# Attention with TensorE's order written out: products in one run, other pieces placed by stated durations

## The chip, the cores and the metric

The kernel runs on one core of one Trainium2 chip. The metric is the time of one execution on the device, in microseconds (us): the median of 9 runs is 1704.61 us (1700.4 to 1714.43). The engines are TensorE (PE for matmuls and PEld for the loads of their weights), VectorE (DVE), ScalarE (ACT), GpSimd (POOL) and SyncE (SP, which issues most of the DMAs here).

## The reference

Two transformer blocks over 8 sequences of 512 tokens and 256 features, all in float32. Each block is a layernorm, causal attention with 16 heads of 16 features, a residual addition, a second layernorm, a router, a mixture of experts and another residual addition. Block 0 has rotary position codes, 4 key/value heads, and 32 experts of which each token takes 8. Block 1 has 16 key/value heads, 16 experts with 2 per token, and a shared expert besides.

```
x = x + attention0(layernorm(x));  x = x + moe0(layernorm(x))
x = x + attention1(layernorm(x));  x = x + moe1(layernorm(x))
attention: softmax(mask(q k^T / 4)) v, then the output projection
moe:       sum over chosen e of weight_e * down_e(silu(gate_e x) * up_e x)
```

## The kernel before

The program has four stages: attention 0 over the 8 sequences, the experts of block 0, attention 1 over the 8 sequences, and the experts of block 1 with the gathering of results. The change touches the two attention stages.

**A sequence's heads.** In `Attention` (L615) the 16 heads go in 4 groups (index c) of 4 heads. For one group, `scores` (L628) writes the transposed scores of three "banks" of key blocks (index n): block 0 (512 columns per head), blocks 1 and 3 together (384 + 128), and block 2 (256). Its matmuls (L638) use 32 rows of TensorE for each head, so four heads run side by side. All three banks use one and the same PSUM tile `st` of 4 of the 8 PSUM banks, so the next scores can only be written after ScalarE's exponential (L643) has read the last. `mask` (L649) multiplies the diagonal blocks with a triangle on VectorE. `values` (L653) multiplies the probabilities with v (L661, 32 columns of TensorE per head, four heads side by side, a column of ones beside v for the softmax sums) in four steps, one for each key block. Then it copies the sums out of PSUM on VectorE (L667), transposes them (L674, tile `ot`), and divides (L677, L678) into `otok`.

**The order.** `steps` (L684) is a generator with 6 steps for a group, 24 for a sequence. At each step it makes one scores bank or one piece of the group's `values` generator; the products trail the scores, so that the steps of one group are spread between the next group's scores. `pipeline` (L734) runs the steps of sequence b, and at each of them takes pieces of two other generators: `before(b + 1)`, the next sequence's layernorm, transposes (`turned`, L302: `xT`) and projections (in stage 0 the transposes of the input `xin` at L1251, then `qkv` at L843 with the rotary products on VectorE at L850 to L865, then the transposes `qT`, `kT`; in stage 1 `v` at L941, `q` at L954, `k` at L959); and `finish(b - 1)`, the last sequence's output projection (`oT` L719, `y` L727, addition L731), layernorm, `xT_f`, router (`lg` L321, `rk` L368 and L370) and, in stage 1, the shared expert (`sg` and `su` L402, `sy` L415). The pieces are spread evenly by their number over the steps. A `yield` ends a piece. What follows is the order in which the program traces its instructions; the framework's own scheduler then chooses each engine's order from it, with estimated durations. On the chip each engine runs that order as it stands.

**What the pieces carry to other queues.** At the end of the router's piece, POOL issues the scatters of the layernormed rows to the experts' slabs (L385: 32 for each sequence in stage 0, 8 in stage 1). They read the tile `xn_rows`, which has 2 buffers in stage 0 and 1 in stage 1, so the layernorm of a later sequence waits until they have landed. In stage 1, `ahead1` (L1418) fetches the x of sequence b + 3 through SP during sequence b and issues 32 gathers on POOL (L1200), a pair for each call of `next(early)`; it needs a buffer of x that is free when an earlier sequence is kept (`keep_x`, SP). Weights of the experts are loaded by SP in the same places.

**The experts' stages** already have TensorE's order written out (`tc.manual_schedule`, L1173 to L1179).

Of the kernel before, what the change touches and what calls it, by code (L numbers as in the profile page):

```python
# [72 lines left out]
STEPS = 2 * len(BANKS)  # L73
# [17 lines left out]
def two_blocks_kernel(  # L91
# [78 lines left out]
    def biases1(tmp, bank):  # L170
# [8 lines left out]
        yield  # L179
# [18 lines left out]
        yield  # L198
# [98 lines left out]
    def free():  # L297

        for _ in range(4):
            yield  # L300

    def turned(xn, lnp, bank, name):  # L302

        xT = lnp.tile([P, ND, T], F32, tag="xT", name=f"xT_{name}")
        for c in range(ND):
# [4 lines left out]
            yield  # L310
        return xT

    def ffn_parts(smp, bank):
        def route(n, b, xn, xT, name, again):
# [10 lines left out]
            yield  # L325
# [11 lines left out]
            yield  # L337
# [10 lines left out]
            yield  # L348
# [15 lines left out]
            yield  # L364
# [26 lines left out]
            yield  # L391

        def shared(w, xT, x, name):

            hs = smp.tile([P, NS, T], F32, tag="hs", name=f"hs_{name}", bufs=1)
            for n in range(NS):
# [11 lines left out]
                yield  # L408
            for half_ in range(NT // 2):
# [11 lines left out]
                yield  # L421
# [193 lines left out]
    class Attention:  # L615
# [6 lines left out]
        def __init__(self, n, late, ptp, ps, bank, wo, masked=None):  # L622
            self.n, self.fine, self.late, self.ptp, self.ps, self.bank, self.wo = n, fines[n], late, ptp, ps, bank, wo
            self.heads, self.otok, self.rec = {}, {}, {}
            self.last = iter(())
            self.masked = masked

        def scores(self, b, c, n, probs):  # L628
# [13 lines left out]
            pt = self.ptp.tile([P, NG, width], F32, tag="p2" if n == 2 else "p01", name=f"p_{name}", bufs=1 + (n < 2))  # L642
# [10 lines left out]
        def values(self, b, c, probs):  # L653
# [4 lines left out]
            for step, j in enumerate((0, 1, 3, 2)):  # L658
# [6 lines left out]
                yield  # L665
            osb = late.tile([P, T], F32, tag="osb", name=f"osb_{name}", bufs=1)
            nc.vector.tensor_copy(osb, o)  # L667
            yield
# [4 lines left out]
            for t in range(NT):  # L673
                nc.tensor.transpose(ot[:, t * P : (t + 1) * P], osb[:, t * P : (t + 1) * P], ident)  # L674
# [7 lines left out]
            yield  # L682

        def steps(self, b):  # L684

# [4 lines left out]
            for c in range(NCK):  # L690
                probs = {}
                for n in range(len(BANKS)):
                    self.scores(b, c, n, probs)
                    next(self.last, None)
                    yield
                    if n == len(BANKS) - 1:
                        self.last = self.values(b, c, probs)
                    next(self.last, None)
                    yield
                    self.mask(n, probs)  # L700

        def flush(self):
            for _ in range(STEPS - 1):
                next(self.last, None)
                yield

        def output(self, b, x):
# [8 lines left out]
            for k in range(ND):  # L716
# [4 lines left out]
                yield  # L721
            for h in range(NT // 2):
# [9 lines left out]
                yield  # L732

    def pipeline(att, before, after, n_before, n_after, till, ahead=None, lead=0):  # L734
# [8 lines left out]

        n_steps = NCK * STEPS
        n_after += 4
        drain(before(0))
        for b in range(NB):
            pre = before(b + 1) if b + 1 < NB else iter(())
            post = finish(b - 1) if b else iter(())
            early = ahead(b + 3) if ahead and b + 3 < NB else iter(())  # L750
            made_pre = made_post = 0
            for n, _ in enumerate(att.steps(b)):
# [932 lines left out]
```

## Time and profile before

| | |
|---|---|
| median of 9 runs | 1704.61 us |
| profiled execution, its own time | 1705.27 us |
| its span, from the first to the last instruction | 1703.5 us |
| mean granted TensorE clock | 0.961 |
| attention 0, first exponential of the first sequence to that of the last | 32.7 to 355.8 us |
| first expert transposes of block 0 | 425 us |
| attention 1, first exponential of the first sequence to that of the last | 888.6 to 1329.9 us |
| first expert transposes of block 1 | 1428 us |

The page gives each engine's busy time; the answers by window give the same for a stretch of the span. The columns of such a row are the stretch, its length, then busy time and instruction count of PE, PEld, DVE, ACT and POOL, then the granted clock of TensorE, the DMA share and GB/s. In what follows the stretches run from the first exponential of one sequence to that of the next, so that their length is the period of a sequence. A row of waits names the engine, its tile and line, what it waited for, and then the total, the number of waits and the longest one.

### The profile page before, as it was taken

What the parts mean: (1) busy time and instruction counts of PE and PEld (TensorE: products, weight loads), DVE (VectorE), ACT (ScalarE), POOL (GpSimd) and SP (SyncE); (2) the same over time, 40 slices, a digit from 0 to 9 for tenths busy, and PEclk for the clock granted to TensorE, in tenths of its full rate; (3) what the DMA queues carried; (4) which work ended last, traced back from release to release, by engine and by line L of the source; (5) the groups of instructions that cost most, each with busy time, mean ns of one, the idle gap of its engine ahead of it and who ended that gap; (6) DMA issues with size and microseconds to landing.
All of it is one profiled execution on the core that took longest, in us unless ns stands there. A gap on an engine that the chain in (4) does not pass through costs nothing. (4 is left out here: it accounts for less than half of the span.)

```text
span 1703.5 us, 30922 instructions
## 1 busy us (share of the span) xinstructions
PE 1548.7 (91%) x10180; PEld 1030.7 (61%) x10180; DVE 992.5 (58%) x3131; ACT 650.2 (38%) x865; POOL 795.9 (47%) x660
## 2 busy tenths in 40 slices
PE   5899999995999999999988999989899888999982
PEld 2355544543898999988853455445444445777761
DVE  5687887875554555555555764754656544444452
ACT  2555554552232333333334454454455331222221
POOL 0026767577710004888888548888511011000473
PEclk9999999997999999999999999999999988999996
DMA  2035557236988768999984245664312024343563
GB/s 73 13 88 154 163 167 265 100 140 197 308 262 271 202 201 220 273 261 274 271 188 69 45 107 82 125 138 69 83 52 79 26 86 156 107 156 119 157 226 120
DMA packets 255129, 259.45 MB, mean 152 GB/s; under 512 B 80212, under 2 KB 235988, under 8 KB 254964
## 3 DMA queue, kind: packets, MB, share of 16 engines
q1 hardware_dynamic: 199172, 167.88, 32.3%
q0 software_dynamic: 55296, 88.65, 22.8%
q8 instruction: 88, 1.44, 0.3%
q10 hardware_dynamic: 496, 0.85, 0.2%
q14 instruction: 77, 0.63, 0.1%
HBM read 132.70 MB, written 124.57 MB: 151 GB/s over the span
## 5 line engine op out<-in xcount | busy, mean ns | idle before, releaser
L1200 POOL DMA_INDIRECT x_a<-yg,yrows x256 | 404.5, 1580 | 277.8 <-DMA xg_m<-xg 181.2
L385 POOL DMA_INDIRECT xg<-xn_f,rows_f x320 | 323.5, 1011 | 413.4 <-DVE rows_f L382 197.2
L643 ACT ACTIVATE p_a<-st_a 128x2048 f32<-128x2048 f32 (+1 forms) x192 | 306.0, 1594 | 280.5 <-PE st_a L638 244.2
L1131 PE MATMUL gu_m<-gw,xgTs_m 128*128 x1552 | 335.9, 360 | 4.9 <-DVE xgTs_m L1108 3.0
L1131 PEld LDWEIGHTS gu_m<-gw,xgTs_m 128*128 128x128 f32 x1552 | 258.1, 192 | 34.2 <-DVE xgTs_m L1108 3.3
L1162 PE MATMUL y_m<-dw,hTs_m 96*128 (+1 forms) x952 | 237.7, 379 | 0.0
L638 PE MATMUL st_a<-qT_a,kT_a 32*128 32x512 f32 (+3 forms) x2048 | 203.2, 479 | 11.2 <-ACT p_a L643 11.0
L661 PE MATMUL o_a<-p_a,v 128*32 128x512 f32 (+3 forms) x2048 | 197.6, 455 | 6.7 <-DVE p_a L649 6.6
L649 DVE TENSOR_TENSOR p_a<-p_a,causal 128x512 f32<-128x512 f32 x256 | 170.4, 684 | 56.8 <-ACT p_a L643 55.9
L1108 DVE COPY xgTs_m<-xgT_m 128x512 f32<-128x512 f32 x194 | 133.8, 690 | 109.9 <-PE xgT_m L1106 109.6
L1167 ACT COPY ys_m<-y_m 128x512 f32<-128x512 f32 x194 | 113.6, 585 | 188.9 <-PE y_m L1162 171.7
L1123 DVE SCALAR_TENSOR_TENSOR h_m<-h_m,xg_m,gu_m 128x96 f32<-128x96 f32 (+1 forms) x388 | 114.9, 326 | 117.4 <-ACT h_m L1136 70.5
L1162 PEld LDWEIGHTS y_m<-dw,hTs_m 96*128 96x128 f32 (+1 forms) x952 | 165.2, 190 | 15.1
L1262 POOL DMA_INDIRECT g<-yg,yrows x64 | 65.1, 1017 | 203.3 <-DVE h_m L1123 171.9
L638 PEld LDWEIGHTS st_a<-qT_a,kT_a 32*128 32x128 f32 x2048 | 90.2, 189 | 107.0 <-issue 51.7
L1152 DVE COPY hTs_m<-hT_m 96x256 f32<-96x256 f32 (+1 forms) x194 | 92.8, 479 | 97.0 <-PE hT_m L1151 96.4
L1106 PE MATMUL xgT_m<-ident,xg_m 128*128 128x128 f32 x776 | 120.1, 277 | 15.1 <-DMA xg_m<-xg 12.1
L1139 ACT ACTIVATE h_m<-gu_m 128x192 f32<-128x192 f32 x150 | 49.5, 330 | 211.3 <-PE gu_m L1131 203.2
L1106 PEld LDWEIGHTS xgT_m<-ident,xg_m 128*128 128x128 f32 x776 | 96.1, 142 | 39.2 <-issue 14.8
L661 PEld LDWEIGHTS o_a<-p_a,v 128*32 128x32 f32 x2048 | 49.6, 110 | 108.8 <-issue 67.1
L1151 PE MATMUL hT_m<-ident,h_m 128*96 128x128 f32 (+1 forms) x476 | 84.6, 274 | 0.4 <-DVE h_m L1123 0.4
L667 DVE COPY osb_a<-o_a 128x512 f32<-128x512 f32 x64 | 44.0, 687 | 53.9 <-PE o_a L661 53.7
(198 smaller groups left out, 1690.9 us busy)
## 6 DMA issues: line engine op xcount, KB each, us to landing
yg<-ys_m SPq DMA_DIRECT2D x194, 256.0 KB
xg_m<-xg SPq DMA_DIRECT2D x300, 144.0 KB
xg_m<-xg SPq DMA_DIRECT2D x88, 136.0 KB
xg<-zeros SPq DMA_DIRECT2D x66, 144.0 KB
xg<-xn_f,rows_f POOLq DMA_INDIRECT x320
xg<-zeros SPq DMA_DIRECT2D x34, 136.0 KB
xf<-in_x_dram SPq DMA_DIRECT2D x8, 512.0 KB
x_after<-x_in SPq DMA_DIRECT2D x8, 512.0 KB
```

The costliest lines, as they stand in the source:

```text
L385: inst = nc.gpsimd.indirect_dma_start(out=lay.xg, out_offset=bass.IndirectOffsetOnAxis(ap=rows[:, t, i : i + 1], axis=0), in_=xn[:, t, :], ...
L638: nc.tensor.matmul(st[:, g, at : at + T - j * P], kT[r, j * P : (j + 1) * P], qT[r, j * P :], start=True, stop=True,)
L643: nc.scalar.activation(pt, st[:, :, :width], AF.Exp, scale=SCALE)
L649: self.masked = nc.vector.tensor_tensor(d, d, causal.unsqueeze(1).to_broadcast([P, NG, P]), ALU.mult).ins
L661: nc.tensor.matmul(o[32 * g : 32 * g + 32, j * P :], v1[:, j, v_at + g * (DH + 1) :][:, :32], probs[n][:, g, at : at + T - j * P], start=( ...
L1106: nc.tensor.transpose(tr[:, j, c, :], xg[:, j, c * P : (c + 1) * P], ident)
L1108: nc.vector.tensor_copy(xT, tr)
L1123: nc.vector.scalar_tensor_tensor(h[:, j, :], h[:, j, :], xg[:, j, D:][:, bass.ds(offs[part, i + j][2], 1)], gus[j][:, inner:], ALU.mult, A ...
L1131: nc.tensor.matmul(gus[j], xT[:, j, c, :], gu[:, bass.ds(at + c * 2 * inner, 2 * inner)], start=(c == 0), stop=(c == ND - 1),)
L1162: nc.tensor.matmul(y[:, j, :], hT[:n_in, q, j, :], dn[:n_in, bass.ds(at + q * D, D)], start=(q == 0), stop=(q == n_ch - 1),)
L1167: nc.scalar.copy(ys, y)
L1200: nc.gpsimd.indirect_dma_start(out=xs[b][:, t, :], out_offset=None, in_=yg, in_offset=rows, compute_op=ALU.add)
```

## The change

- The steps of a sequence become 12 gaps (4 groups of 3 banks). In gap 0 of a group TensorE gets the scores of bank 0 and behind them all four products of the group before, in one run (`products`); in gap 1 the scores of bank 1 and the `ot` transposes (`normalize`); in gap 2 the scores of bank 2. The copy of the products out of PSUM moves from VectorE to ScalarE. The tile of probabilities of banks 0 and 1 gets 3 buffers in place of 2.
- Each piece of `before` and `finish` yields a duration. Negative ones stand for waiting and bring no work. A class `Fill` shares a part's total over its gaps by fixed shares and takes pieces while a part is behind or a gap has less than a least amount of work (`LEAST`).
- `finish(b - 1)` begins in gap 2 of sequence b and ends in gap 1 of sequence b + 1. The gathers of `ahead` are called twice in each gap from gap 2, in place of once in each of 24 steps.
- In stage 1 the shared expert's pieces go between the router's, and `qT` and `kT` become single tiles with 3 buffers.
- The whole attention pipeline traces under `tc.manual_schedule(engines={ENG.PE})`, so TensorE's order is the program's; the other engines' orders are still chosen by the framework's scheduler.

```diff
-STEPS = 2 * len(BANKS)
+NGAP = NCK * len(BANKS)
+LEAST = (0.0, 1.6, 1.2)
...
     def free():
         for _ in range(4):
-            yield
+            yield -0.75
...
-            pt = self.ptp.tile([P, NG, width], F32, tag="p2" if n == 2 else "p01", name=f"p_{name}", bufs=1 + (n < 2))
+            pt = self.ptp.tile([P, NG, width], F32, tag="p2" if n == 2 else "p01", name=f"p_{name}", bufs=3 if n < 2 else 1)
...
-                yield
-            osb = late.tile([P, T], F32, tag="osb", name=f"osb_{name}", bufs=1)
-            nc.vector.tensor_copy(osb, o)
-            yield
+            self.osb = late.tile([P, T], F32, tag="osb", name=f"osb_{name}", bufs=1)
+            nc.scalar.copy(self.osb, o)
+
+        def normalize(self, b, c, probs):
...
                 for n in range(len(BANKS)):
                     self.scores(b, c, n, probs)
-                    next(self.last, None)
-                    yield
-                    if n == len(BANKS) - 1:
-                        self.last = self.values(b, c, probs)
-                    next(self.last, None)
+                    if self.last:
+                        (self.products, self.normalize, lambda *_: None)[n](*self.last)
                     yield
                     self.mask(n, probs)
+                self.last = (b, c, probs)
...
+    class Fill:
+        def __init__(self, part, total, share, first, last):
+            self.part, self.total, self.first, self.last = part, total, first, last
+            whole = sum(share[k % len(BANKS)] for k in range(first, last + 1))
+            self.share = [total * s / whole for s in share]
+            self.gap = -1
+            self.at = self.due = 0.0
+            self.waits = False
+        def pass_gap(self, n):
+            self.gap += 1
+            if self.gap >= self.first:
+                self.due += self.share[n]
+        def behind(self):
+            return (self.due - self.at) / self.total
+        def able(self):
+            return self.part and self.gap >= self.first and (self.behind() > 0.0 or not self.waits)
+        def make(self):
+            cost = next(self.part, None)
+            if cost is None:
+                self.part = ()
+                return 0.0
+            self.waits = cost < 0.0
+            self.at += abs(cost)
+            return max(cost, 0.0)
...
+        with tc.manual_schedule(engines={ENG.PE}):
+            drain(before(0))
+            fills = []
+            for b in range(NB):
+                if b:
+                    last = NGAP + 1 if b + 1 < NB else NGAP - 1
+                    fills.append(Fill(finish(b - 1), t_after(b - 1), share, 2, last))
+                if b + 1 < NB:
+                    fills.append(Fill(before(b + 1), t_before, share, 0, NGAP - 2))
+                early = ahead(b + 3) if ahead and b + 3 < NB else iter(())
+                for k, _ in enumerate(att.steps(b)):
+                    filled = 0.0
+                    for fill in fills:
+                        fill.pass_gap(k % len(BANKS))
+                    while True:
+                        able = [f for f in fills if f.able()]
+                        if not able:
+                            break
+                        fill = max(able, key=lambda f: f.behind())
+                        if fill.behind() <= 0.0 and filled >= LEAST[k % len(BANKS)]:
+                            break
+                        filled += fill.make()
+                    for fill in [f for f in fills if f.gap > f.last]:
+                        drain(fill.part)
+                        fills.remove(fill)
+                    if k > 1:
+                        next(early, None)
+                        next(early, None)
+                drain(early)
+            for fill in fills:
+                drain(fill.part)
+            att.flush()
+            drain(finish(NB - 1))
...
-        pipeline(att, before, after0, 15, 12, 22)
+        pipeline(
+            att, before, after0, 12.7, lambda b: 13.5 + (b == 1) + 5.0 * (b == SPLIT[0] - 1), (0.05, 0.55, 0.4)
+        )
...
-                yield from route(1, b, xn, xT, name, False)
-                yield from shared(w1["s"], xT, xs[b], name)
+                routed, beside = route(1, b, xn, xT, name, False), shared(w1["s"], xT, xs[b], name)
+                for made in (routed, beside, routed, routed, beside, routed, routed):
+                    yield next(made)
+                drain(routed)
+                yield from beside
...
-            pipeline(att, before, after1, 15, 17, NCK * STEPS, ahead1, 4)
+            pipeline(
+                att, before, after1, 15.1, lambda b: 29.2 + 4.0 * (b == SPLIT[1] - 1), (0.25, 0.42, 0.33), ahead1
+            )
```

The other yields carry these durations: `xin`, `xT`, `oT`, `qT`, `kT` and each step of the experts' tables 0.5; `qkv` 1.4; halves of `y` and `v`, and each `q` and `k` 1.75; `lg` 1.9; `rk` with the scatters 0.3; a shared expert's `sg` and `su` 3.5, half of `sy` 2.6; waits of 0.6 after `xT`, 1.0 after `oT`, 0.4 between the router's pieces on VectorE, and four times 0.75 for a layernorm.

## The prediction

> **What bounds the kernel now.** I first read the waits by stage, then the rows by window (a sequence from its first exponential to the next one's), then TensorE in order of time. The chain of what ended last reaches back only to 1665 us, into the gathering of results, which the change leaves alone.
>
> ```profile
> 76.10:121.10 45.00, 42.59 (x374) 22.69 (x375) 37.20 (x136) 25.17 (x25) 3.61 (x3) 1.00 0.25 66
> 167.40:213.50 46.10, 43.66 (x388) 23.18 (x388) 37.36 (x136) 25.29 (x24) 32.52 (x33) 1.00 0.51 159
> 262.20:312.00 49.80, 47.09 (x374) 23.99 (x370) 34.07 (x130) 25.36 (x25) 28.80 (x28) 0.97 0.58 200
> 312.00:355.80 43.80, 43.59 (x392) 23.04 (x389) 39.47 (x146) 25.19 (x24) 32.65 (x32) 1.00 0.37 130
> ```
> ```profile
> 1060.94:1123.99 63.05, 61.14 (x420) 31.57 (x419) 39.24 (x127) 31.09 (x28) 52.37 (x36) 1.00 0.60 115
> 1123.99:1193.62 69.63, 63.66 (x420) 33.21 (x419) 39.39 (x127) 31.10 (x29) 57.74 (x40) 0.95 0.59 111
> ```
> PE is busy nearly all of each sequence; POOL fills up in attention 1. The last two rows have the same work: the 6.6 us between them are a wait of xT_f (4.96 us, at 1151.11) and a clock of 0.95.
>
> ```profile
> PE xT_f L308 <- DVE xn_f L292: 14.9, 6, 6.2
> ...
> DVE xn_f L292 <- DMA xg<-xn_f,rows_f: 9.5, 2, 5.4
> ```
> These waits are of attention 1 (935 and 890 to 1330): TensorE waits for xn_f, and xn_f waits for the scatter of the sequence before, whose source it overwrites.
>
> ```profile
> 167.29 1.06 PE L661 MATMUL o_a<-p_a,v 128*32 128x384 f32 x14
> 168.29 0.65 PE L1251 MATMUL xin<-ident,xf 128*128 128x128 f32 x4
> 168.87 0.64 PE L661 MATMUL o_a<-p_a,v 128*32 128x256 f32 x8
> 169.44 0.66 PE L1251 MATMUL xin<-ident,xf 128*128 128x128 f32 x4
> 170.03 1.15 PE L638 MATMUL st_a<-qT_a,kT_a 32*128 32x384 f32 x16
> 171.11 0.66 PE L674 MATMUL ot_a<-ident,osb_a 128*128 128x128 f32 x4
> 171.69 1.07 PE L661 MATMUL o_a<-p_a,v 128*32 128x512 f32 x8
> 172.69 0.66 PE L719 MATMUL oT_a<-ident,otok_a 128*128 128x128 f32 x4
> 175.58 0.30 PE L719 MATMUL oT_a<-ident,otok_a 128*128 128x128 f32 x1 [2.24 <-DVE otok_a L678]
> ```
> Read the starts: four transposes between products take 0.58 us. Within a run they follow at 0.107 (0.43 for four), 256-column matmuls at 0.2145. So each stretch of whole-array work between four-head pieces costs 0.15 to 0.2 beyond its columns.
>
> **The terms.** On PE: scores 1.07, 1.08 and 0.64 (start to start). Products alone 1.00 (512 columns), 0.78, 0.36 and 0.57 (256); 384 and 128 joined take 1.00, so a join saves 0.14 and the run of four takes 2.71 - 0.42 = 2.3. A y or v half, q or k 1.72; qkv 1.28; lg 1.8; sg with su 3.43; sy half 2.6; 0.43 for four transposes; 0.2 for each whole-array stretch. A gap can't be shorter than its exponential lets the one score tile come free: scores, 0.2, exponential (1.88, 1.88, 1.02 by its rows), 0.1: 3.24, 3.24, 1.95.
>
> Working the placement rule by hand with the change's own durations gives the gaps of a full sequence (longer of the two limits).
> Attention 0: 4.0 (half xin), 3.24, 1.95 (two oT), 3.4, 5.6 (two xT, half y, a qkv), 3.8 (half y, a qkv), 3.4, 4.3 (two qkv), 2.1 (three of xT, qT, kT), 3.4, 4.4 (lg and the other two), 1.95: 41.5 us. Six such sequences now take (355.8 - 76.1)/6 = 46.6.
> Attention 1: 3.4, 4.3 (half sy), 4.3 (oT, xT_a, half y), 7.0 (half v, half y), 3.4 (half v), 3.4 (xT_f, q), 5.6 (lg), 6.9 (sg/su, k), 6.0 (q, sg/su), 5.3 (k), 5.4 (rk, sg/su), 3.4 (half sy): 58.4, against 63.05.
>
> **What goes.** oT's wait of about 2.1 a sequence (otok queued behind a layernorm): otok now comes a gap earlier. The products' waits for the mask (PEld, 23.8 us over 50 waits in all): scores and three products now lie ahead of the late one. What is late next is in the following terms.
>
> **New waits, attention 0.** TensorE takes each piece in its place, and behind a late one stand the next scores, hence ACT and DVE too.
> (a) Two qkv stand in gap 7, qT in gap 8. From the end of y on, VectorE owes a layernorm (5.0 us when alone: y ends 1395.5, xT_f starts 1400.60), three rotary tiles at 1.75, one mask 0.62, rec and otok 0.6: 11.5 us, while PE gets from y to qT in 9.2. I take 2.3, with 0 (rotary ahead of the layernorm) and 5 (masks in front, the 39.47 row's load) as ends.
> (b) lg directly behind xT_f waits for two copies (0.584 each) that stand behind an exponential: 1.8 in every second sequence, 0.9; ends 0 and 1.8.
> (c) xT_a three gaps after its layernorm, and small ones: 1.1 (the tables' small steps of sequence 4 among them); ends 0 and 3.
> Sum 45.8 a sequence, 0.8 less than now, 5 us over six. The first sequence has little to fill: 36.3 by gaps and 2 of (a), against 43.4: 5 us less. The last: 2.5 less. Attention 0: **-12.5**.
> The osb copy's move takes 0.69 x 4 from VectorE and gives 0.59 x 4 to ACT, which is idle 45% of a sequence; it must end before ot, about 1.1 us after the products. If it doesn't, 0 to 0.6 a group, inside (c)'s end. The third probability tile lets the exponential of bank 0 run before the products free the first; without it gap 0 would take 2.3 more. qT and kT with 3 buffers only free sooner; TensorE's order hides that either way.
> POOL's 32 scatters take 42 us a sequence (32 x 1.3), so 45.8 still covers them; with two xn_rows buffers a lag has a sequence of slack. SP's weight loads move with the scatters, for a stage that begins after 400 us: nothing, and at most the 8 us of the first xg load if they were late.
>
> **Attention 1.** (d) xT_a, y behind four ACT copies in gap 2: 1.2 (0 to 2.5). (e) xT_f stands one gap (4.3 us) behind y, the layernorm needs 5.0 alone and some 2 of v additions and masks come between: 3 (1 to 5).
> The first sequence has 40.2 by gaps and 1 of waits, against 46.1: -5. The second 57.3 + 4.2 against 63.1: -1.6.
> Sequences 2 to 5 are bound by POOL. From 1004.6 to 1219.9 it runs without a pause: three times 32 gathers at 1.9 (1.6 and 0.3 of issue) and 8 scatters at 1.3, 214 us. They begin 6.7 us after sequence 2's start (997.9), when sequence 0's x is kept. In the new order that is kept in gap 1 of sequence 2 and the fetch goes out in gap 2, so they begin at some 13 (estimate: gap 2 starts at 7.7, keep and fetch 5.3); 15 of 16 pairs still precede the scatter, so it ends at 13 + 214 - 4 = 223 (now 222). xT_f of sequence 4 follows at 225.5 (now 224.1), then 35 of sequence 5 remain (now 41): sequence 6 starts 260.6 after sequence 2, against 265.4: -4.8. TensorE's gain in these sequences becomes waiting for POOL.
> Sequence 6: 64 with the tables against 66.6; the last +1 (its layernorm has no cover); the drained tail -3, since sg/su now stands where rk waited (2.81 us). Attention 1: **-16**.
> ACT's table loads (1.283 each, 30 now) rise to about 42, as three silus each stand between exponentials: 15 us of ACT, beside 31 of 63 busy; only gap 11 (3.7 against 3.4) shows it, 0.3 a sequence, inside (d).
>
> Sum: 1705.3 (the profiled execution, 1703.5 of span) - 28.5 = 1677; the median of the runs, 1704.6, is 0.7 lower.
>
> [...] The row first: the clock was 1.00 in the sequence with a wait of 2.24 us and 0.95 in that with 4.96, where 1.6 us went beyond the wait. [...]
>
> **Rivals.**
> 1. *The waits are covered* (VectorE's scheduler puts rotary tiles first): attention 0 41.5 a sequence, -31 - 7 - 2.5 = -40; attention 1 without (d) and (e), sequences 2 to 5 still held by POOL, -6 - 6 - 5 - 5 - 3 = -25: **1640**. For it: VectorE is idle 8 us of 46. Against: it is late exactly where two qkv and a layernorm meet.
> 2. *VectorE late in the fixed order, slower*: (a) 5, (b) 1.8, (c) 2, and 1.5 of clock for each long idle time: 51.8 a sequence, +23 in attention 0; (e) at 5 in four sequences, -8 in attention 1: **1720**. It decides when the three waits pass 9 us a sequence. For it: VectorE is busy 39.47 of 43.8 in the fastest sequence.
> 3. *No change in time*: the waits come to what switching saves, 1704.
>
> **Chances.** Forecast 0.46 (own range 1660 to 1696), rival 1 0.20, rival 2 0.24, rival 3 0.10. The range takes in most of rivals 1 and 2: 1638 to 1722. No change means within 0.3%, 5 us, what a measurement tells here: faster 0.44 + 0.20 + 0.02 = 0.66, same 0.08, slower 0.26.
>
> **What would show it.** Attention 0's period about 46, its gaps 0 and 3 near 3.4; qT waiting for the rotary sum (kr, qr) on VectorE; xT_f in attention 1 waiting 3 us in early sequences and more behind POOL; L1200 starting some 13 us into sequence 2; the experts' stages unchanged. I would be wrong if VectorE's order puts a layernorm's writing of xn, which itself waits for POOL, ahead of masks, or if the periods fall to 41.

## The result and the profile after

The changed kernel takes 1719.33 us in the median of 10 runs (1716.6 to 1723.4), the kernel before 1703.25 in 31: a ratio of 1.0089 with a 95% interval of 1.0074 to 1.0104. It is 16 us slower, where 28 less were forecast, and it ends at the time of the second rival (1720). The profiled executions are 1705.27 and 1716.86 us (spans 1703.5 and 1715.1); every stretch below is from their traces, from start to start.

Cut at the first and last scores of each attention and at the experts' first transposes and last matmul, the two spans are (us):

| stretch | before | after | difference | forecast |
|---|---|---|---|---|
| to the first scores | 31.5 | 30.5 | -1.0 | 0 |
| attention 0, first to last scores | 361.0 | 360.3 | -0.7 | -12.5 |
| tail of attention 0, to the experts | 32.9 | 40.0 | +7.1 | no term |
| experts 0 | 443.3 | 444.9 | +1.6 | 0 |
| from the experts to attention 1's first scores | 17.8 | 21.8 | +4.0 | no term |
| attention 1, first to last scores | 493.9 | 502.1 | +8.2 | -13 |
| tail of attention 1 | 47.9 | 42.9 | -5.0 | -3 |
| experts 1 and results | 275.4 | 272.6 | -2.8 | 0 |

Two stretches that cost 11 us had no term at all, and both attentions miss what was forecast for them. A single stretch is no better known than to some 3 us: the two runs below that keep one attention in exactly the instruction order of before took 364.4 us for attention 0 and 490.4 for attention 1. Rows by sequence of the changed kernel (columns as in the rows of before: stretch and length, then busy time of PE, PEld, DVE, ACT, POOL, then the granted clock):

```profile
72.00:117.75 45.75, 41.25 (x368) 23.25 (x368) 34.65 (x123) 27.28 (x29) 0.00 (x0) 0.95 0.23 58
117.75:161.60 43.85, 40.90 (x376) 23.41 (x378) 33.56 (x124) 27.25 (x28) 25.92 (x25) 0.97 0.46 142
256.40:308.60 52.20, 45.33 (x368) 24.09 (x367) 32.74 (x123) 27.49 (x29) 34.98 (x35) 0.89 0.63 215
308.60:355.90 47.30, 42.62 (x376) 23.92 (x375) 35.59 (x132) 27.23 (x28) 28.58 (x28) 0.93 0.30 107
1066.70:1134.50 67.80, 61.23 (x420) 33.47 (x424) 37.34 (x124) 35.96 (x34) 56.21 (x39) 0.95 0.61 114
1134.50:1205.00 70.50, 63.84 (x420) 35.05 (x422) 37.32 (x124) 36.06 (x34) 58.30 (x41) 0.90 0.58 110
```

PE's busy time did fall: 41.25 us in the first of these, 42.59 in the row of before, and 42.62 in the last of attention 0 against 43.59. Over the six full sequences of attention 0 it fell by 0.7 to 3.0 us each, which fits the pieces in one go saving switches. But five of these six sequences got longer (45.0, 46.4, 49.8, 43.8, 63.1 and 69.6 us before), and the clock, 0.95 to 1.00 in them before, is now 0.89 to 0.97. TensorE is less busy, waits more, and runs slower. The waits of the changed kernel, and below them one of the kernel before (who waits for whom: us in all, times, longest):

```profile
PE xT_f L311 <- DVE xn_f L293: 36.4, 18, 6.9
PE st_a L642 <- ACT p_a L647: 30.4, 24, 3.0
...
PE qT_a L921 <- DVE qr_a L905: 7.4, 7, 1.6
...
PE lg_f L325 <- ACT xT_f L312: 4.5, 6, 1.0
```

```profile
PE st_a L638 <- ACT p_a L643: 11.0, 12, 3.0
```

The wait for scores by way of the exponential (`st_a`) was 11.0 us in 12 places before, `xT_f`'s 30.2 in 11. `qT_a`'s wait is new, and `lg_f`'s was 0.3 in one place.

### The profile page after: what moved, and what is told of

Same layout as the page of the kernel before. It is cut to its first block, busy times and chain, and to the rows that moved or that the text cites. A ratio compares the mean times of both kernels' runs of the same rounds, so it can differ in the third digit from the quotient of the medians.

```text
span 1715.1 us, 30906 instructions
## 1 busy us (share of the span) xinstructions
PE 1526.8 (89%) x10180; PEld 1048.9 (61%) x10180; DVE 959.4 (56%) x3067; ACT 704.0 (41%) x943; POOL 793.8 (46%) x660
## 3 DMA queue, kind: packets, MB, share of 16 engines
q0 software_dynamic: 55296, 88.65, 22.5%
## 5 line engine op out<-in xcount | busy, mean ns | idle before, releaser
L665 PE MATMUL o_a<-p_a,v 128*32 128x512 f32 (+3 forms) x2048 | 164.8, 466 | 0.0
L665 PEld LDWEIGHTS o_a<-p_a,v 128*32 128x32 f32 x2048 | 60.2, 116 | 129.0 <-issue 116.5
L1155 PE MATMUL xgT_m<-ident,xg_m 128*128 128x128 f32 x776 | 120.1, 277 | 16.1 <-DMA xg_m<-xg 12.0
L1200 PEld LDWEIGHTS hT_m<-ident,h_m 128*96 128x96 f32 (+1 forms) x476 | 58.5, 125 | 18.9 <-issue 7.5
```

The costliest lines, as they stand in the source:

```text
L665: nc.tensor.matmul(o[32 * g : 32 * g + 32, j * P :], v1[:, j, v_at + g * (DH + 1) :][:, :32], probs[n][:, g, at : at + T - j * P], start=( ...
L1155: nc.tensor.transpose(tr[:, j, c, :], xg[:, j, c * P : (c + 1) * P], ident)
L1200: nc.tensor.transpose(hp[:n_in, q, j, :], h[:, j, lo : lo + n_in], ident)
```

## Experiments

The first four ran on a chip on which the kernel before took 1702.87 us. All later ones came to chips on which it took 2010 to 2029 us ("disturbed" in what follows; what is known of it stands at the end); their ratios stand to the kernel before on the same chip, and there only stretches are read that the disturbance leaves alone.

**Which stage loses.** Two kernels with one attention in the changed order and the other exactly as before, down to each engine's order of instructions.

```diff
# new_in_a0: attention 1 keeps the pipeline and classes of before
-            pipeline(att, before, after1, 15.1, ..., (0.25, 0.42, 0.33), ahead1)
+            pipeline_old(att, before, after1, 15, 17, NCK * STEPS, ahead1, 4)
# new_in_a1: attention 0 keeps them
-        pipeline(att, before, after0, 12.7, ..., (0.05, 0.55, 0.4))
+        pipeline_old(att, before, after0, 15, 12, 22)
```

> Attention 0 in the changed order, attention 1 wholly as before. Theory 'the ends': in the profiled executions the last scores of attention 0 come 1.6 us earlier than before, and from the last scores to the experts' first transposes it takes 39.9 us against 32.9, so this kernel is 5 to 6 us slower than before (ratio 1.003 to 1.004), with the whole loss in that drained tail. Rival 'late VectorE in the sequences': the loss of the changed kernel (about 16 us by the medians) lies in attention 0's sequences and this kernel shows most of it, 10 us or more. Rival 'attention 1 alone': no difference from before within 3 us.

> Attention 1 in the changed order, attention 0 wholly as before. Theory 'the ends and POOL': 4 us more before the first scores (the layernorm of sequence 0), 8 us more over the sequences (POOL's gathers start at 16.8 us into sequence 2 instead of 6.7), 5 us less in the drained tail: 6 to 9 us slower than before (ratio 1.004 to 1.005). Rival 'attention 0 alone': no difference within 3 us. If the two stages add up, this kernel and the one with attention 0 alone changed come to some 12 to 16 us together.

Measured: 1709.72 us, ratio 1.0043 (1.0026 to 1.0060), and 1713.14, ratio 1.0049 (1.0032 to 1.0066). The first has its sequences at 360.9 us and its tail at 40.0: attention 0's whole loss is the tail. The second has 21.7 before attention 1, 504.9 in it, 43.3 behind it. The profile of the second is of its longest run, 1719.44 us. The losses by ratio, 0.43 and 0.49%, add up to the whole, 0.89%, within their intervals; neither stage alone is the cause.

**The tail of attention 0.** TensorE before the change, from the last scores on (start, busy time, engine, line, operation; in brackets the idle time and what ended it):

```profile
392.11 0.71 PE L638 MATMUL st_a<-qT_a,kT_a 32*128 32x256 f32 x8 [1.05 <-ACT p_a L643]
392.83 1.07 PE L661 MATMUL o_a<-p_a,v 128*32 128x384 f32 x16
394.69 0.64 PE L661 MATMUL o_a<-p_a,v 128*32 128x256 f32 x8 [0.79 <-DVE p_a L649]
396.15 0.66 PE L674 MATMUL ot_a<-ident,osb_a 128*128 128x128 f32 x4 [0.82 <-DVE osb_a L667]
...
398.11 3.69 PE L727 MATMUL y_a<-wo,oT_a 128*128 128x256 f32 x16
407.29 2.12 PE L308 MATMUL xT_f<-ident,xn_f 128*128 128x128 f32 x8 [5.49 <-DVE xn_f L292]
```

and after it:

```profile
390.44 0.71 PE L642 MATMUL st_a<-qT_a,kT_a 32*128 32x256 f32 x8
393.93 0.21 PE L372 MATMUL rk_f<-chosen,upper 128*128 128x32 bf16 x2 [2.78 <-DVE chosen L354]
...
395.76 0.19 PE L374 MATMUL rk_f<-before_f,ones 128*128 128x32 bf16 x1 [0.71 <-DVE before_f L367]
395.88 4.50 PE L665 MATMUL o_a<-p_a,v 128*32 128x512 f32 x32
401.13 0.66 PE L680 MATMUL ot_a<-ident,osb_a 128*128 128x128 f32 x4 [0.76 <-ACT osb_a L670]
...
404.01 3.29 PE L731 MATMUL y_a<-wo,oT_a 128*128 128x256 f32 x14 [0.24 <-ACT oT_a L723]
412.25 2.21 PE L311 MATMUL xT_f<-ident,xn_f 128*128 128x128 f32 x8 [4.96 <-DVE xn_f L293]
```

Before, the first products follow the scores at once. After, sequence 6's ranking stands ahead of them and waits 2.78 us for VectorE's choice of experts, then 0.71 for a sum; and the 32 products take 4.50 us where they take 2.36 elsewhere. The granted clock was 0.50 from 394 to 400.5 us, and 1.00 in the same place before (392 to 402 us). `ot` comes 10.4 us behind the last scores instead of 3.7, and everything down to the experts hangs on it.

The first attempt to undo that missed:

```diff
+            att.flush()
             for fill in fills:
                 drain(fill.part)
-            att.flush()
```

> The changed kernel with the last group's products and normalization put ahead of what is left of the sequence before it, in both stages. Theory 'the ends': in the tail of attention 0 TensorE stood 2.78 us at the ranking of sequence 6 with the last products queued behind it, and ot came at 401.1 instead of some 396; the tail gets 5 us shorter, that of attention 1 0 to 2 us, so 5 to 7 us less than the changed kernel (ratio to before 1.005 to 1.006). Rival 'the clock': the products were slow for a lowered clock after an idle time, and the idle time only moves; the tail of attention 0 stays within 2 us of 39.9.

Measured: 1719.78 us, ratio 1.0087, tail 40.2. The expectation failed for a plain reason: the ranking had already been made within the last gap, so nothing was left for the flush to pass. The next edit keeps it out of that gap as well:

```diff
-                    last = NGAP + 1 if b + 1 < NB else NGAP - 1
+                    last = NGAP + 1 if b + 1 < NB or att.n == 0 else NGAP - 1
...
+            att.flush()
             for fill in fills:
                 drain(fill.part)
-            att.flush()
```

> The changed kernel with one piece moved in attention 0's drained tail: the ranking of sequence 6 (which waits for VectorE's choice of experts) comes behind the last group's products and normalization instead of ahead of them. (The run before this that put the flush first moved nothing there: the ranking had already been made in the last gap.) Theory 'idle and clock': of the tail's 40.0 us 6 to 7 are the ranking's waits (2.8 and 0.7) and products that then run at 4.5 us for 32, twice their usual 2.3; the products now start 0.7 us after the last scores as before the change, and the tail falls to 33 to 35. As sequence 6's logits then stand directly behind their transposes in gap 10, 0 to 2 us come back in the sequences: 4 to 6 us less than the changed kernel in all. Rival 'VectorE': the products wait for the last mask, which VectorE makes after the choice of experts; the tail stays above 38.

It ran on a disturbed chip (ratio 1.0095, 1.0057 to 1.0132; in a repeat 1.0064, 1.0037 to 1.0092). There the tail as a whole can't be read, since the kernel before with other buffers takes 61.5 and 63.6 us for it on such chips instead of 32.9. But up to the last of `y` the new order without this edit takes 16.0 to 17.1 us there in seven profiles, as on the first chip (16.1):

```profile
608.87 0.91 PE L642 MATMUL st_a<-qT_a,kT_a 32*128 32x256 f32 x8
609.71 3.80 PE L665 MATMUL o_a<-p_a,v 128*32 128x512 f32 x32
614.28 0.66 PE L680 MATMUL ot_a<-ident,osb_a 128*128 128x128 f32 x4 [0.77 <-ACT osb_a L670]
...
617.26 3.29 PE L731 MATMUL y_a<-wo,oT_a 128*128 128x256 f32 x14 [0.24 <-ACT oT_a L723]
```

The products start 0.5 us behind the last scores and the last of `y` 11.0 (repeat: 0.6 and 10.8), against 5.1 and 16.1 in the changed kernel and 0.4 and 9.0 before. So 5 of the 7 us go with the order, as theory had it; the products still take 3.8, at a granted clock of 0.56 (609 to 611 us). The rival, that the products wait for the last mask, fell.

> The same kernel as the run before with the ranking behind the last products, on a chip whose instruction and data transfers aren't slowed. On the slow chip the products started 0.5 us behind the last scores and y ended 11.3 us behind them (changed kernel: 16.3). Theory 'idle and clock': the tail falls from 40.0 to 35 to 36, 4 to 5 us less than the changed kernel in the profile, less 0 to 2 in the last sequence. Rival 'VectorE': above 38.

That transfers were slowed on the disturbed chips is a guess of this and later expectations; what the traces show of it stands at the end.

**The start of attention 1.** VectorE after the change, behind the experts' last copies, and the transposes that wait for it:

```profile
874.64 0.74 DVE L288 BATCH_NORM_STATS2 stats_a<-x_a 128x6 f32<-128x256 f32 x2
...
880.51 1.01 DVE L830 MEMSET v<- 128x1148 f32 x1 [0.19 <-issue]
...
882.64 1.23 DVE L293 TENSOR_SCALAR xn_a<-x_a,mv_a,rstd_a 128x256 f32<-128x256 f32 x4
```

```profile
882.93 2.33 PE L311 MATMUL xT_a<-ident,xn_a 128*128 128x128 f32 x8 [6.91 <-DVE xn_a L293]
```

In the new order sequence 1's first work is made in gap 0, ahead of the first mask, so its layernorm has the same release as sequence 0's; VectorE alternates between the two (the trace from 876.5 on). Besides, its order now has two memsets of `v` ahead of `xn_a` (880.5 and 881.7), which before stood behind it (`xn_a` at 871.9, the first memset at 873.6). `xn_a` begins 8.0 us behind the first statistics instead of 4.3; 2.3 of these 3.7 us are the memsets. `xT_a` waits 6.91 us, where it waited 3.35 before:

```profile
872.37 1.53 PE L308 MATMUL xT_a<-ident,xn_a 128*128 128x128 f32 x8 [3.35 <-DVE xn_a L292]
```

The edit makes that first work from gap 1 on, behind the mask:

```diff
-                    fills.append(Fill(before(b + 1), t_before, share, 0, NGAP - 2))
+                    fills.append(Fill(before(b + 1), t_before, share, int(att.n == 1 and b == 0), NGAP - 2))
```

> The changed kernel with sequence 1's first work in attention 1 (its layernorm) made in gap 1 instead of gap 0 of sequence 0, so behind the first mask. Theory 'two layernorms share VectorE': in the changed kernel the statistics of sequences 0 and 1 have the same release and alternate on VectorE from 874.6 on, and xT_a waits 6.91 us instead of 3.35; with sequence 1's behind the first mask, the stretch from the experts' last matmul to the first scores falls from 21.8 to 17.8 to 19, 3 to 4 us less. Rival 'the two memsets and x': VectorE's memsets of the v tiles (1.01 us each, ahead of xn_a) and the layernorm itself hold it: 21 or more, no gain.

```profile
1150.09 2.43 PE L311 MATMUL xT_a<-ident,xn_a 128*128 128x128 f32 x8 [3.65 <-DVE xn_a L293]
```

Measured: 2023.40 us, ratio 1.0076 (1.0050 to 1.0103). The stretch falls to 17.7 us (other kernels in the new order without the edit, same kind of chip: 20.3 to 21.7; the kernel before with other buffers: 18.1 and 19.0), the wait to 3.65. That is the 4 us. The edit took both causes away at once, since with it the memsets stand behind `xn_a` again:

```profile
1149.62 1.51 DVE L293 TENSOR_SCALAR xn_a<-x_a,mv_a,rstd_a 128x256 f32<-128x256 f32 x4
1151.32 1.01 DVE L830 MEMSET v<- 128x1148 f32 x1 [0.19 <-issue]
```

So the rival was wrong that no gain would come, but right that the memsets hold `xn_a`: theirs is the larger share, and only their place ahead of it goes back to sequence 1's early layernorm. (In the kernel with only attention 0 changed the stretch was 19.1, so some 1 us of it varies by itself.)

**The sequences of attention 0.** TensorE in gap 10 of sequence 1 and on into the next:

```profile
109.31 1.04 PE L311 MATMUL xT_f<-ident,xn_f 128*128 128x128 f32 x8
111.37 2.24 PE L325 MATMUL lg_f<-rw,xT_f 128*128 128x32 f32 x16 [1.01 <-ACT xT_f L312]
113.53 0.87 PE L642 MATMUL st_a<-qT_a,kT_a 32*128 32x256 f32 x8
115.59 2.09 PE L642 MATMUL st_a<-qT_a,kT_a 32*128 32x512 f32 x8 [1.18 <-ACT p_a L647]
117.61 3.91 PE L665 MATMUL o_a<-p_a,v 128*32 128x512 f32 x32
```

The logits wait 1.01 us for ScalarE's copy of `xT_f`, the small scores come late, so their exponential is late, so the next scores wait 1.18; and then scores and products run at half speed (2.09 for eight scores, 3.91 for 32 products). The clock in these stretches:

```profile
109.00:114.50 5.50, 4.31 (x36) 3.36 (x35) 2.56 (x6) 3.01 (x4) 0.00 (x0) 0.95 0.00 0
114.50:117.75 3.25, 2.16 (x12) 0.66 (x16) 3.03 (x21) 1.04 (x3) 0.00 (x0) 0.50 0.00 0
117.75:120.50 2.75, 2.75 (x16) 0.65 (x18) 0.87 (x2) 1.88 (x1) 0.00 (x0) 0.50 0.02 6
120.50:123.25 2.75, 2.75 (x41) 1.70 (x34) 0.49 (x2) 1.08 (x2) 0.00 (x0) 0.95 0.00 0
```

Sequence 2 is the control within the same trace: by the placement rule one `qT` and one `kT` stand around its logits, the copy is done in time, and about the same wait for the exponential costs no clock (granted 1.00 from 154 to 167 us):

```profile
158.44 0.71 PE L642 MATMUL st_a<-qT_a,kT_a 32*128 32x256 f32 x8
160.40 1.14 PE L642 MATMUL st_a<-qT_a,kT_a 32*128 32x512 f32 x8 [1.24 <-ACT p_a L647]
161.47 1.80 PE L665 MATMUL o_a<-p_a,v 128*32 128x512 f32 x17
```

Gap 10, gap 11 and the next gap 0 together, from exponential to exponential: 14.3, 14.2, 14.4 and 14.1 us in sequences 1, 3, 5 and 6, each with a wait of 1.01 and the clock at 0.50 behind it, and 10.2 in sequence 2. (Before: 9.5 to 10.0. Sequence 4, whose gaps hold the experts' tables besides, took 15.2, and 12.4 before.) The edit gives the logits a place of their own:

```diff
             xT = yield from turned(xn, lnp, bank, name)
+            yield -0.8
             yield from route(0, b, xn, xT, name, False)
```

> The changed kernel with a waiting place of 0.8 between xT_f and the logits in attention 0, so that by the placement rule the logits of sequences 1, 2, 3 stand in gap 11, a gap behind their transposes, instead of directly behind them in gap 10. Theory 'logits behind the copies': where both stand in gap 10 it takes 5.55 to 6.4 us from exponential to exponential instead of 3.96, the next scores then wait 1.5 for a late exponential, and the clock falls (products 0.4 us apart instead of 0.2) into the next gap 0; the sequences concerned get 2 to 3.5 us shorter, attention 0 8 to 12 us in all (360.3 to 348 to 352). Rival 'the wait moves': the exponential chain or the ranking, now a gap later, holds TensorE instead, and attention 0 stays within 3 us of 360.3.

```profile
114.59 1.04 PE L311 MATMUL xT_f<-ident,xn_f 128*128 128x128 f32 x8
116.17 0.71 PE L642 MATMUL st_a<-qT_a,kT_a 32*128 32x256 f32 x8 [0.54 <-ACT p_a L647]
116.81 2.07 PE L325 MATMUL lg_f<-rw,xT_f 128*128 128x32 f32 x16
118.81 1.14 PE L642 MATMUL st_a<-qT_a,kT_a 32*128 32x512 f32 x8
119.88 2.36 PE L665 MATMUL o_a<-p_a,v 128*32 128x512 f32 x32
```

```profile
117.00:120.00 3.00, 3.00 (x28) 2.18 (x31) 1.49 (x4) 1.32 (x3) 0.00 (x0) 1.00 0.00 0
120.00:122.00 2.00, 2.00 (x32) 0.77 (x29) 1.93 (x18) 1.88 (x1) 0.00 (x0) 1.00 0.04 8
```

The logits stand behind the small scores, only the small scores still wait, 0.54 us, the clock stays at 1.00, and the three gaps take 9.7 us. In the six profiles with this edit, alone or with the others, they take 9.7 in sequences 3 and 5 throughout, and in sequence 1 four times (11.4 twice); without it on the same kind of chip 14.4 and 14.2 in sequences 1 and 3. Sequence 1, which no scatter disturbs, takes 43.3, 43.8 and 43.8 us in the three runs of this edit and 43.3 to 43.7 in three of the four edits together, against 45.8 to 47.3 in ten profiles of the new order without it. Attention 0 as a whole: 560 to 566 us with the edit alone, 569 to 584 in six profiles without it on such chips, 13 us less by their means. The ratios were 1.0054 (1.0024 to 1.0085), 1.0010 (0.9991 to 1.0029) and 1.0032 (1.0012 to 1.0052); the other single edits had 1.0076 to 1.0095, 1.0036 to 1.0064 and 1.0068 on the same three chips. The rival, that the wait only moves, fell. How much of the 13 us an undisturbed chip gives wasn't measured; the first trace's own control puts it at four times 4 us.

> The logits' place alone. Theory: attention 0 takes 347 to 352 us instead of 360.3, with gap 10 at 2.7 in sequences 1, 3, 5 and 6, and nothing else changes: ratio to before 1.002 to 1.004. Rival 'the wait moves': attention 0 within 3 us of 360.3, ratio 1.008 or more.

**POOL in attention 1.** From the trace's rows of POOL, and of SP's keep and fetch of x:

```
                 sequence 2   x kept at   gathers from   third scatter ends   sequence 6
before                997.9      997.5         1004.6               1219.9       1263.3
after                1004.0     1013.9         1020.8               1233.7       1274.7
gathers from gap 0   1005.1          -   (no pause: 32 follow on the ones before, to 1028.7)   1285.0
```

```profile
1013.86 0.34 SPq L161 DMA_DIRECT2D x_after<-x_a  x1
1016.54 0.34 SPq L164 DMA_DIRECT2D x_a<-x_after  x1
```

Sequence 0's x is kept 9.9 us into sequence 2, when its last addition is done; keep and fetch take 7.0 more, and the gathers begin 16.8 us into the sequence instead of 6.7. The obvious cure:

```diff
-        xs[b] = xpool.tile([P, NT, D], F32, tag="x", name=f"x_{name}_{b}", bufs=5)
+        xs[b] = xpool.tile([P, NT, D], F32, tag="x", name=f"x_{name}_{b}", bufs=6)
...
-                    if k > 1:
-                        next(early, None)
-                        next(early, None)
+                    next(early, None)
+                    next(early, None)
```

> The changed kernel with the fetch of x and the gathers of attention 1 from gap 0 of a sequence instead of gap 2 (and a sixth buffer for x, so that the fetch needn't wait for x of an earlier sequence to be kept). Theory 'POOL sets sequences 2 to 5': the gathers begin at 5 to 8 us into sequence 2 instead of 16.8, the third group of scatters ends 9 to 11 us earlier, and sequence 6 starts some 260 us after sequence 2 instead of 270.7: 8 to 10 us less than the changed kernel (ratio to before 1.003 to 1.004). Rival 'TensorE's own waits set them': the waits of xT_f at 6 to 8 us shrink, but others take their place, and the stretch stays within 3 us of 270.7.

Measured: 1727.72 us, ratio 1.0146 (1.0123 to 1.0170), 8 us slower than the changed kernel, with 508.8 us in attention 1. Both theories fell. POOL was early: its last 32 gathers ended at 1169.7 instead of 1223.5. But the gathers now stood ahead of sequence 0's scatter, which began at 1029.0 instead of 998.1, and the next layernorm couldn't overwrite the scatter's source:

```profile
DVE xn_f L293 <- DMA xg<-xn_f,rows_f: 11.5, 1, 11.5
```

TensorE's `xT_f` waited 12.0 us there and sequence 2 took 75.3 us instead of 62.7. In sequences 3 and 4 it waited 6.9 and 6.8 us more for the same. So an earlier POOL alone gains nothing while a scatter stands behind 32 gathers (60 us). The changed kernel has the same wait in its slow sequences (1066 to 1215 us; 6.1 more in the sequence behind them), and the kernel before had it in two:

```profile
DVE xn_f L293 <- DMA xg<-xn_f,rows_f: 8.5, 2, 4.3
```

Another cure left the question open: two buffers for these rows, in the changed kernel and in the one before.

```diff
-                xn = layernorm(xs[b], lnp, name, "xn_rows", 1, E1)
+                xn = layernorm(xs[b], lnp, name, "xn_rows", 2, E1)
```

> The changed kernel with two buffers instead of one for the normalized rows that attention 1 scatters, so that a layernorm needn't wait until the scatter of the sequence before has read them. Theory 'the scatter queued behind 32 gathers': xT_f's waits of 6.0, 6.1 and 8.1 us in sequences 3 to 5 fall to the 2.1 of the others, and sequence 6 starts 252 to 258 us after sequence 2 instead of 270.7: 12 to 18 us less than the changed kernel, about the time before the change or less. Rival 'POOL's sum': gathers and scatters take 71 us of POOL in each of three sequences, so another transfer or wait (the keys' buffers, the fetch of x) takes the place of this one and the stretch stays above 265.

> The kernel before with two buffers for the rows that attention 1 scatters, and nothing else. If the scatter behind the gathers is a cost that was there before the change: xT_f's waits of 5 to 6 us in sequences 4 and 5 go, sequence 6 starts 252 to 254 us after sequence 2 instead of 265.4, 11 to 13 us less (ratio 0.992 to 0.994). If POOL's sum sets it: no difference beyond 3 us.

All on disturbed chips. In the changed order the longest idle time before `xT_f` in sequences 2 to 6 was 1.9, 2.1 and 1.7 us. But of six profiles on such chips without the second buffer only two had a long one at all (8.1 and 5.9 us; 0.8 to 2.5 in the others), so that the edit had little to take away there. Sequences 2 to 5 came to 269.2, 274.9 and 269.6, against 273.6 to 282.6 in those six: 5 us, not 12 to 18 (ratios 1.0079, 1.0036, 1.0068). In the kernel before the buffer changed nothing (0.9993 and, repeated, 0.9991, interval 0.9976 to 1.0007); that kernel wasn't profiled on such a chip without the buffer. What the wait for the scatter costs on an undisturbed chip wasn't settled.

**The four edits together** (the ranking behind the products, the later layernorm, the logits' place, the row buffers), three times on such chips:

> The changed kernel with four single edits together: the ranking behind the last products, sequence 1's layernorm of attention 1 behind the first mask, the logits a gap behind their transposes, two buffers for the scattered rows. Theory 'each wait is a place in the order': the gains add up, 4 + 3 + 8 to 12 + 12 to 18 less than the changed kernel, so 1682 to 1692 where the changed kernel takes 1719 and the one before 1703 (ratio 0.987 to 0.994). Rival 'TensorE in a fixed order is held by VectorE and ScalarE wherever a piece is put': less than half of it, 1705 or more (ratio 1.001 or more).

> The four edits together, read by stretch, if the chip's transfers are of the first speed. Theory 'each wait is a place in the order': attention 0 346 to 352 us (changed kernel 360.3), its tail 35 to 36 (40.0), start of attention 1 18 (21.8), attention 1 484 to 490 (502.1); in all 1680 to 1692, ratio to before 0.986 to 0.994. Rival 'a fixed order is held wherever a piece is put': attention 0 above 357 and attention 1 above 497, 1705 or more.

2011.77, 1999.29 and 2018.30 us; ratios to the kernel before 0.9924 (0.9896 to 0.9952), 0.9943 (0.9924 to 0.9962), 0.9944 (0.9921 to 0.9966). The start of attention 1 took 18.0, 18.2 and 18.0 us, `y` ended 11.4 to 12.9 us behind the last scores, sequences 2 to 5 of attention 1 took 263 to 274. So the fixed order with these edits is 0.6 to 0.8% faster than the kernel before on those chips, at or just above the upper end of what theory had, where every kernel in the new order with one of them was between 0.1 and 0.95% slower (one interval takes in no change). The changed kernel without any edit wasn't run there. The rival, that a fixed order is held wherever a piece is put, fell. On a chip as the first the four together weren't run.

## Why the prediction was wrong

By its own steps:

- *Products in one go, fewer switches*: right. 32 products take 2.36 us (2.3 was taken), PE's busy time fell by 0.7 to 3.0 us in each full sequence of attention 0, and the products' wait for masks fell from 23.8 us to 1.6.
- *(a) qT waits for VectorE, 2.3 a sequence*: right in kind, half in size: 7.4 us in seven places. In sequence 5 it came together with `kT`'s wait and a lower clock (0.89 over the sequence, 52.2 us).
- *(b) lg behind two copies, 0.9 a sequence*: this term failed in attention 0. The wait itself was 1.0; what was left out is what it starts, a late exponential (1.2) and half clock through the next scores and products. It came to 4.0 us in four of six sequences, 16 us where 5.4 were entered. These 10.6 us are more than the 9 by which the six full sequences missed (283.9 us; forecast 275, before 279.7). The edit that gave the logits a place of their own took the 4 us away.
- *The clock*: the forecast entered no loss of clock at the logits. The second rival's 1.5 us for each long idle time is an estimate from one row of before (6.6 us between two sequences, less a wait of 4.96). Here shorter waits went with a larger loss: no wait in gap 10 was over 1.32 us, and the clock fell to 0.50 for 6.8 us. It did so in all four sequences whose logits waited 1.01 us: within the logits in sequence 3 (at 202.7 us), at the small scores in 1 and 5 (114.0 and 305.1), and in the wait of 1.32 behind them in 6 (352.9). In sequence 2, with the same logits that waited for nothing and one wait of 1.24 us behind them, it stayed at 1.00. What decides wasn't tested.
- *The first sequence -5, the last -2.5*: -3.2 and -1.8.
- *Stretches without a term*: the tail of attention 0 (+7.1) and the start of attention 1 (+4.0). Both follow from the order that the diff writes out: a finish that comes to its ranking in the last gap, and a layernorm made before the first mask, with two memsets that came ahead of the first `xn_a` along with it. The first could have been read from the placement that was worked out for the gaps, and the second's common release too; the working stopped at the full sequences.
- *Attention 1, the first sequence -5, the second -1.6*: -4.8 and -0.1.
- *(c) 1.1 a sequence, (d) 1.2 a sequence*: `xT_a` waited 1.2 us once in the six sequences of attention 0, and the tables' small steps 2.7 in sequence 4. In attention 1 `xT_a` and `y` hardly waited; in their place `oT` waited 1.5 in five sequences for an addition on VectorE.
- *POOL starts at some 13 us and 15 of 16 pairs precede the scatter*: it started at 16.8 (x is kept at 9.9 us, not 7.7; keep and fetch took 7.0, not 5.3), and all 32 gathers preceded it. The third scatter ended 229.7 us into sequence 2 (223 forecast) and sequence 6 started 41.0 behind that (37.6 forecast), 270.7 us after sequence 2, where 260.6 were forecast and 265.4 measured before: a miss of 10 us. "Bound by POOL" holds only in part: with the third scatter over 50 us earlier these sequences took 279.9.
- *(e) xT_f 3 us*: the idle time before `xT_f` came to 1.3, 1.3 and 1.1 us in sequences 1, 2 and 6; in 3 to 5, behind the scatter, to 4.9, 5.1 and 7.0. (The expectations have 2 for the former and 6.0, 6.1 and 8.1 for the latter, about 1 us more than the trace's idle time.)
- *Sequence 6 at 64 us, the last +1, the tail -3*: 69.0, +5.5 and -5.0. What left the tail came back in the last sequence, whose `xT_f` waited 5.7 us without cover (2.7 before), at a clock of 0.88. Sequence 6 had no wait over 1.5 us; why it took 5 us more than forecast stays open.
- *ScalarE's table loads 30 to 42*: 30 to 44 in attention 1; no wait of TensorE by them is seen.

Of the 40 us between forecast and profile, 11 are the two stretches without a term, 12 attention 0's sequences (10.6 entered too little for the logits), 10 sequences 2 to 5 of attention 1, 11 its other sequences; its tail and the stages that the change leaves alone take off 2 each. For the first two shares single edits show the cause. For attention 1's sequences, 8 us slower than before the change, no edit does: the account of POOL and the scatter is read from the traces. The second rival had the time right, but not its working: it put +23 us into attention 0's sequences, where the loss was none, and -8 into attention 1.

## What to carry to other kernels

When TensorE's order is written out by hand, work out its two ends with the same care as its steady state: what stands ahead of the last products, and what is released together with the first layernorm and may go ahead of it, cost 11 us here, while the sequences between gained nothing in attention 0 and lost 8 us in attention 1. In a fixed order put at least one piece that waits for nothing between a transpose and the matmul that reads its copy, since a wait of 1 us there became 4 here. And a shorter queue time for one kind of transfer isn't a gain if it moves ahead of another kind that releases a buffer (here a layernorm waited 11.5 us for its scatter): ask which transfer each engine needs next, not which can go first.

## What the runs showed of the hardware

In the changed kernel's trace the granted clock fell to 0.50 behind idle times of TensorE of 1.01 to 2.78 us. Between 74 and 402 us the stretches at 0.50 began at 114.0, 202.7, 250.5, 291.5, 305.1, 352.9 and 393.9 us. At 114.0, 202.7, 305.1 and 352.9 the logits had waited 1.01 us (at 352.9 the next wait, of 1.32, was under way), at 250.5 a count of the experts' tables 2.00 and at 291.5 `qT` 1.64; at 393.9 the wait of 2.78 ahead of the ranking was just ending. Each stretch lasted 6.83 us, and the distances of their starts (88.7, 47.8, 41.0, 13.7, 47.8 and 41.0) are 26, 14, 12, 4, 14 and 12 times half of that. In the trace of before the three stretches at 0.50 between 72 and 402 us, from 129.9, 222.1 and 297.2 us, lasted 3.41 us each. So in these sequences of the changed kernel a wait either cost no clock at all, as the 1.24 us of sequence 2, or was followed by 6.83 us at half clock.

On the four other chips that the later experiments came to, the kernel before was 18 to 19% slower (2010 to 2029 us against 1703). In sequences 2 to 6 of attention 0 ScalarE stood without work for long, in one profile with the logits apart for up to 33.0, 17.6, 26.3, 21.9 and 23.6 us at a time. In sequence 2 its operand had been there all the while; the profile names no releaser on the chip ("remote"). ScalarE in that sequence of the kernel with the logits apart (120 to 195 us):

```profile
ACT osb_a L670 <- remote: 33.0, 1, 33.0
```

TensorE's matmuls came one in 1 to 3 us meanwhile and then stopped too, and both went on 5 to 6 us after the last of the 32 scatters had been issued (171.6 us). On the first chip no such wait is seen beside the same scatters. The experts' stages were longer as well, 473 to 481 and 294 to 300 us against 443 to 446 and 273 to 275. The expectations call this slowed transfers; that isn't shown, since the packets of the two largest DMA queues took about the same time in all (by their shares of the span, 27.2 and 19.3%, some 550 and 390 us with the ranking behind the products; 549 and 386, from 32.0 and 22.5%, in the changed kernel on the first chip). The cause stays open.
